# Attention scores for four heads at a time, in four row groups and four PSUM banks

## The chip, the cores and the metric

The kernel runs on one core of a Trainium2 chip. The metric is the device time in microseconds (us) of one execution. A profile is taken in an execution of its own. TensorE (PE in the profile) does matmuls and transposes into PSUM, which has eight banks of 2 KB per partition; VectorE (DVE) and ScalarE (ACT) read the banks and do the elementwise work; GpSimd (POOL) does elementwise work and gathers; SyncE (SP) issues transfers.

## The reference, cut to what matters

One block of a gated cross-attention layer, over 8 batches of 256 rows with 512 columns:

```python
x = x + tanh(g_xattn) * xattn(layernorm(x), ctx, mask, ...)
x = x + tanh(g_ffn) * ffn(layernorm(x), ...)

# xattn: 16 heads of 32 columns; q and the output go through int8-quantised products
q = w8a8_linear(x, wq, bq)      # heads: B, 16, 256, 32
k = cond @ wk.T + bk            # B, 16, 256, 32
v = cond @ wv.T + bv
scores = q @ k.T / sqrt(32) + mask
o = softmax(scores) @ v
return w8a8_linear(o, wo, bo)
```

The feed-forward part quantises its input and weights to an fp8 grid, with permuted columns, and computes `silu(g) * u` and a product down. The change touches only the attention.

## The kernel before

The program is written as a sequence of operations on tiles; a planner lays out each engine's queue from it, with priorities that follow the program's order, a cost of its own for each operation, and the buffers of each pool; it also sets the semaphores. A queue runs strictly in the order that was laid out. `tc.keep_in_program_order` pins an instruction behind the one written before it on its engine; that keeps an order, but doesn't keep other instructions out from between. `tc.high_priority()` raises the priority of what is written inside it.

First come the weights' transposes and quantisation and the projections of batch 0 (up to about 60 us), then the eight batches of attention (to about 560 us), then the feed-forward part, which uses PSUM pools of its own.

For each batch, `attention` walks over NP = 8 pairs of heads in a pipeline of turns. In turn i it writes down:

- `scores(i)`: for both heads of pair i and both row tiles of 128 queries, one matmul of K = 32 rows (a head's 32 columns lie on 32 partitions, so a head occupies one of four row groups of the array), with 256 keys as output columns. Both heads' scores go into one PSUM slot `s` of two banks, a bank per head; the pool `ps_s` has one such slot. Then, per head and row tile, VectorE adds the mask, writes `sn` and takes the row's extreme (L537), and ScalarE writes the exponentials `pr` with their sum (L547). `sn` has two buffers, `pr` four.
- `transposed(i - 1)`: per head four transposes of `pr` (L563) into a bank of the pool `ps_t` (two banks), and a copy to `pT` by VectorE for even heads (L572), by ScalarE for odd ones (L570).
- `weighted(i - 2)`: products of `v` and `pT` (L583) into a bank of `ps_o`, 32 output partitions per head; after every second pair `normalised` transposes and scales four heads' results (L596 to L605).
- a share of the list `others`.

`others` is the side work of the batch, handed out evenly over the 11 turns: the previous batch's output projection and its quantisation for the feed-forward part (`project_out`, `quantise_x2`), the next batch's projections (`project_kv` with the lines L414 to L445, `project_q` with L462 to L493), and pieces of the feed-forward weights' preparation (`prep_up`, `prep_down`; the helpers at L162 to L184 and L281 to L284). All that these write on TensorE goes through `bank`, the pool `ps_m` of three banks. So PSUM is split into 2 banks for scores, 2 for transposes of the exponentials, 1 for weighted sums and 3 for everything else.

Of the kernel before, what the change touches and what calls it, by code (L numbers as in the profile page):

```python
# [29 lines left out]
F32 = mybir.dt.float32  # L30
# [7 lines left out]
PSUM = bass.MemoryType.PSUM  # L38
DRAM = bass.MemoryType.DRAM

P = 128
# [10 lines left out]
def tile_flamingo_block(  # L52
# [133 lines left out]
    with ExitStack() as actx:  # L186
# [3 lines left out]
        at = actx.enter_context(tc.tile_pool(name="at", bufs=2))  # L190
# [1 line left out]
        one = actx.enter_context(tc.tile_pool(name="one", bufs=1))  # L192
        sm = actx.enter_context(tc.tile_pool(name="sm", bufs=4))
        ps_s = actx.enter_context(tc.tile_pool(name="ps_s", bufs=1, space=PSUM))
        ps_t = actx.enter_context(tc.tile_pool(name="ps_t", bufs=2, space=PSUM))
        ps_o = actx.enter_context(tc.tile_pool(name="ps_o", bufs=1, space=PSUM))
        ps_m = actx.enter_context(tc.tile_pool(name="ps_m", bufs=3, space=PSUM))

        def bank(name, dt=F32):
            n = 512 if dt == F32 else 1024  # L200
            return ps_m.tile([P, n], dt, tag="m", name=name)
# [84 lines left out]
        def load_rows(n, w, tag):  # L286

            tiles = []
            for k in range(KC):
                wr = at.tile([P, C], F32, tag=tag, name=f"wr_{n}{k}", bufs=4)  # L290
# [208 lines left out]
        def attention(b, qT, kT, v, mk, others):  # L499
# [7 lines left out]
            probs, probsT, poT = {}, {}, {}  # L507
            NP = H // 2
            PPC = HPC // 2

            def in_turn(first, ins):

                if not first:
                    tc.keep_in_program_order(ins)

            def scores(i):
                heads = (2 * i, 2 * i + 1)
                both = ps_s.tile([P, 2, TPB, L], F32, tag="s", name=f"s_{b}_{i}")
                pss = {h: both[:, h % 2] for h in heads}
                for nt in range(TPB):  # L520
                    for h in heads:
                        oc, r0 = h // HPC, (h % HPC) * D
                        ins = nc.tensor.matmul(  # L523
                            pss[h][:, nt, :],
                            qT[r0 : r0 + D, oc, nt * P : (nt + 1) * P],
                            kT[r0 : r0 + D, oc, :],
                            start=True,
                            stop=True,
                        )
                        in_turn(nt == 0 and h == heads[0], ins)  # L530
                for h in heads:
                    sn = at.tile([P, TPB, L], F32, tag="sn", name=f"sn_{b}_{h}")
                    pr = at.tile([P, TPB, L], F32, tag="pr", name=f"pr_{b}_{h}", bufs=4)
                    nm = sm.tile([P, TPB], F32, tag="nm", name=f"nm_{b}_{h}")

                    for nt in range(TPB):
                        nc.vector.tensor_tensor_reduce(  # L537
                            out=sn[:, nt, :],
                            in0=pss[h][:, nt, :],
                            in1=mk[:, nt, :],  # L540
                            scale=-1.0,
                            scalar=3.0e38,
                            op0=ALU.add,
                            op1=ALU.min,
                            accum_out=nm[:, nt : nt + 1],
                        )
                        nc.scalar.activation(  # L547
                            pr[:, nt, :],
                            sn[:, nt, :],
                            AF.Exp,  # L550
                            bias=nm[:, nt : nt + 1],
                            scale=-1.0,
                            accum_out=sums[:, nt, h : h + 1],
                        )
                    probs[h] = pr

            def transposed(i):
                for h in (2 * i, 2 * i + 1):
                    pr = probs.pop(h)
                    pst = ps_t.tile([P, LC, S], F32, tag="t", name=f"t_{b}_{h}")  # L560
                    for nt in range(TPB):
                        for lc in range(LC):
                            nc.tensor.transpose(  # L563
                                pst[:, lc, nt * P : (nt + 1) * P],
                                pr[:, nt, lc * P : (lc + 1) * P],
                                ident,
                            )
                    pT = at.tile([P, LC, S], F32, tag="pT", name=f"pT_{b}_{h}", bufs=4)
                    if h % 2:
                        nc.scalar.copy(pT, pst)  # L570
                    else:
                        nc.vector.tensor_copy(pT, pst)  # L572
                    probsT[h] = pT

            def weighted(i):
                heads = (2 * i + 1, 2 * i)
                oc = i // PPC
                if i % PPC == 0:
                    poT[oc] = ps_o.tile([P, S], F32, tag="o", name=f"poT_{b}_{oc}")
                for lc in range(LC):  # L580
                    for h in heads:
                        r0 = (h % HPC) * D
                        ins = nc.tensor.matmul(  # L583
                            poT[oc][r0 : r0 + D, :],
                            v[:, lc, h * D : (h + 1) * D],
                            probsT[h][:, lc, :],
                            start=(lc == 0),
                            stop=(lc == LC - 1),
                        )
# [124 lines left out]
        kT, v, steps = project_kv(0, cr)  # L714
# [3 lines left out]
        qT, q_steps = project_q(0)  # L718
# [215 lines left out]
```

## Time and profile before

| | us |
|---|---|
| median of 3 runs | 800.9 (799.37 to 805.62) |
| the profiled execution | 801.53 |
| its span, from the first to the last instruction | 799.8 |
| TensorE, matmuls | 624.2 busy (78%), 3560 records |
| TensorE, weight loads | 381.3 busy (48%) |
| VectorE | 537.3 busy (67%) |
| ScalarE | 414.3 busy (52%) |
| GpSimd | 279.3 busy (35%) |
| mean granted TensorE clock | 0.86 |

In the lines of the profile, a group of instructions is given as line, engine, operation, output<-inputs, then shapes and count; behind the first bar stand its busy time in us (overlapping instructions counted once) and the mean ns of one; behind the second the idle time of the engine just before the group, and what ended most of it. A row of 40 digits cuts the span into slices of 20 us; a digit is the busy share in tenths. In a table of windows a row is a stretch of the span with its length, the busy time of each engine in it and the number of its instructions, the granted clock, the transfers' share and GB/s. In a timeline a row gives start and duration in us, then the instructions merged.

### The profile page before, as it was taken

What the parts mean: (1) busy time and instruction counts of PE and PEld (TensorE: products, weight loads), DVE (VectorE), ACT (ScalarE), POOL (GpSimd) and SP (SyncE); (2) the same over time, 40 slices, a digit from 0 to 9 for tenths busy, and PEclk for the clock granted to TensorE, in tenths of its full rate; (3) what the DMA queues carried; (4) which work ended last, traced back from release to release, by engine and by line L of the source; (5) the groups of instructions that cost most, each with busy time, mean ns of one, the idle gap of its engine ahead of it and who ended that gap; (6) DMA issues with size and microseconds to landing.
All of it is one profiled execution on the core that took longest, in us unless ns stands there. A gap on an engine that the chain in (4) does not pass through costs nothing. (4 is left out here: it accounts for less than half of the span.)

```text
span 799.8 us, 10417 instructions
## 1 busy us (share of the span) xinstructions
PE 624.2 (78%) x3560; PEld 381.3 (48%) x3584; DVE 537.3 (67%) x1427; ACT 414.3 (52%) x959; POOL 279.3 (35%) x241
## 2 busy tenths in 40 slices
PE   3781798799898898899999889785576686777862
PEld 3640465555465465475575465453263343344431
DVE  3952776848747757756764766995566679778871
ACT  3441964656564665574483475674224544435540
POOL 3523343251141342143121310033545665564531
PEclk9885898998799899799699799678598989989986
DMA  9722130120022220021010411131110010010000
GB/s 290 251 15 12 36 104 27 28 65 14 2 80 85 74 82 25 1 66 41 0 54 14 145 39 46 39 100 47 36 31 26 27 40 27 27 40 27 27 14 26
DMA packets 27157, 42.59 MB, mean 53 GB/s; under 512 B 6528, under 2 KB 14080, under 8 KB 27104
## 3 DMA queue, kind: packets, MB, share of 16 engines
q1 hardware_dynamic: 18656, 29.17, 11.3%
q0 software_dynamic: 4864, 12.22, 5.8%
q10 hardware_dynamic: 3584, 0.54, 0.4%
q8 instruction: 28, 0.46, 0.2%
q14 instruction: 25, 0.20, 0.1%
HBM read 31.28 MB, written 10.63 MB: 52 GB/s over the span
## 5 line engine op out<-in xcount | busy, mean ns | idle before, releaser
L547 ACT ACTIVATE pr<-sn,nm 128x256 f32<-128x256 f32 x256 | 127.4, 499 | 115.8 <-DVE nm L537 91.9
L523 PE MATMUL s<-kT,qT 32*128 32x256 f32 x512 | 99.0, 473 | 44.7 <-DVE nm L537 40.2
L563 PE MATMUL t<-ident,pr 128*128 128x128 f32 x512 | 94.0, 321 | 23.6 <-ACT pr L547 10.8
L537 DVE CUSTOM_DVE_ANT_0 sn<-s,mk 128x256 f32<-128x256 f32 x256 | 96.6, 416 | 15.6 <-PE s L523 14.2
L523 PEld LDWEIGHTS s<-kT,qT 32*128 32x128 f32 x512 | 55.2, 216 | 79.1 <-DVE nm L537 39.4
L563 PEld LDWEIGHTS t<-ident,pr 128*128 128x128 f32 x512 | 66.6, 163 | 51.8 <-ACT pr L547 32.6
L824 PEld LDWEIGHTS <-xg 128*128 128x128 bf16 x512 | 52.6, 104 | 74.8 <-issue 34.9
L856 POOL TENSOR_TENSOR tt<-up,sl 128x704 f32<-128x704 f32 x32 | 62.9, 1966 | 39.6 <-DVE up L846 24.1
L583 PE MATMUL poT<-pT,v 128*32 128x256 f32 x512 | 73.0, 408 | 0.0
L824 PE MATMUL p_up<-upT,xg 128*128 128x352 bf16 x256 | 51.9, 340 | 21.1 <-DVE up L846 18.5
L424 PE MATMUL pk<-cT,wkT 128*128 128x256 f32 x256 | 58.7, 383 | 2.5 <-ACT cT L417 2.5
L824 PE MATMUL p_gate<-gateT,xg 128*128 128x352 bf16 x256 | 48.8, 335 | 14.2 <-DVE gs L837 7.4
L664 POOL TENSOR_TENSOR x_sb<-x_sb,bo_b 128x512 f32<-128x512 f32 x16 | 23.1, 1453 | 101.9 <-ACT xq L462 101.8
L438 PE MATMUL pv<-wvT,cT 128*128 128x512 f32 x128 | 57.1, 598 | 0.2 <-ACT wvT L268 0.2
L665 POOL TENSOR_TENSOR x_sb<-x_sb,y 128x512 f32<-128x512 f32 x16 | 20.2, 1270 | 97.2 <-DVE y L661 65.8
L493 POOL TENSOR_SCALAR qT<-qT,bq_c 128x256 f32<-128x256 f32 x32 | 19.0, 603 | 99.3 <-DVE qT L490 98.9
L424 PEld LDWEIGHTS pk<-cT,wkT 128*128 128x128 f32 x256 | 47.4, 190 | 12.0 <-ACT cT L417 4.2
L184 DVE TENSOR_REDUCE mxt<-tt 128x1 f32<-128x1408 f32 x16 | 25.9, 1619 | 33.9 <-POOL tt L856 33.9
L547 ACT ACTIVATION_READ_ACCUMULATOR pr<-sn,nm 128x1 f32 x256 | 48.0, 188 | 0.0
L572 DVE COPY pT<-t 128x512 f32<-128x512 f32 x64 | 43.7, 683 | 3.4 <-PE t L563 2.8
L874 PE MATMUL yp<-wdT,qtT 128*128 128x512 bf16 x161 | 41.5, 405 | 5.2 <-ACT qtT L871 3.1
L871 ACT COPY qtT<-ptq 128x1024 bf16<-128x1024 bf16 (+1 forms) x32 | 22.3, 749 | 42.8 <-PE ptq L868 42.8
(184 smaller groups left out, 1187.5 us busy)
## 6 DMA issues: line engine op xcount, KB each, us to landing
cr<-in_ctx_dram SPq DMA_DIRECT2D x8, 512.0 KB, 3.9
x_sb<-in_x_dram SPq DMA_DIRECT2D x8, 512.0 KB, 8.5
out_dram<-yo SPq DMA_DIRECT2D x16, 256.0 KB, 2.0
wd<-in_L_ffn_w_down_dram SPq DMA_DIRECT2D x4, 704.0 KB, 4.0
mk<-in_mask_BxSxS_ff_dram SPq DMA_DIRECT2D x8, 256.0 KB, 2.6
scr_x<-x2T SPq DMA_DIRECT2D x8, 256.0 KB, 4.0
scr_gate<-gateT SPq DMA_DIRECT2D x1, 1408.0 KB, 5.2
scr_up<-upT SPq DMA_DIRECT2D x1, 1408.0 KB
```

What stands on the lines that cost most here:

```text
L184: nc.vector.tensor_reduce(dst, src, AX.X, ALU.max, apply_absolute_value=True)
L424: nc.tensor.matmul(pk[:, :L], wTf["k"][:, cc, oc * P : (oc + 1) * P], cT[:, cc, :], start=(cc == 0), stop=(cc == KC - 1),)
L438: nc.tensor.matmul(pv, cT[:, cc, lt * P : (lt + 1) * P], wTf["v"][:, cc, :], start=(cc == 0), stop=(cc == KC - 1),)
L523: ins = nc.tensor.matmul(pss[h][:, nt, :], qT[r0 : r0 + D, oc, nt * P : (nt + 1) * P], kT[r0 : r0 + D, oc, :], start=True, stop=True,)
L537: nc.vector.tensor_tensor_reduce(out=sn[:, nt, :], in0=pss[h][:, nt, :], in1=mk[:, nt, :], scale=-1.0, scalar=3.0e38, op0=ALU.add, op1=ALU ...
L547: nc.scalar.activation(pr[:, nt, :], sn[:, nt, :], AF.Exp, bias=nm[:, nt : nt + 1], scale=-1.0, accum_out=sums[:, nt, h : h + 1],)
L563: nc.tensor.transpose(pst[:, lc, nt * P : (nt + 1) * P], pr[:, nt, lc * P : (lc + 1) * P], ident,)
L572: nc.vector.tensor_copy(pT, pst)
L583: ins = nc.tensor.matmul(poT[oc][r0 : r0 + D, :], v[:, lc, h * D : (h + 1) * D], probsT[h][:, lc, :], start=(lc == 0), stop=(lc == LC - 1),)
L824: nc.tensor.matmul(ph[n][:, j, :QI], xg[:, k, nt * P : (nt + 1) * P], wT[n][:, k, c0 : c0 + QI], start=(k == 0), stop=(k == KC - 1),)
L856: nc.gpsimd.tensor_tensor(tt[:, cols], up, sl, ALU.mult)
L874: nc.tensor.matmul(py, qT[:, k, :], wdT[:, k, :], start=(k == 0), stop=(k == IC - 1))
```

## The change

The pool of two transpose banks is given up; `s` becomes a slot of four banks, still a single one; the transposes take banks from the pool of three. `scores(i)` now covers four heads, which lie in the four row groups, and is called in every second turn. The products of a run go through a new `in_turn`: the first is written as it comes, all later ones at high priority and pinned behind each other. `weighted` uses the same `in_turn`, with two heads as before. Transposes come two turns after the turn of their pair instead of one, the weighted sums three instead of two, and there are 12 turns instead of 11. `pr` gets six buffers. `load_rows`, which loads wv and wq into the buffers of `pT` and `pr`, takes the number of buffers as an argument.

```diff
         ps_s = actx.enter_context(tc.tile_pool(name="ps_s", bufs=1, space=PSUM))
-        ps_t = actx.enter_context(tc.tile_pool(name="ps_t", bufs=2, space=PSUM))
         ps_o = actx.enter_context(tc.tile_pool(name="ps_o", bufs=1, space=PSUM))
         ps_m = actx.enter_context(tc.tile_pool(name="ps_m", bufs=3, space=PSUM))
...
-            def in_turn(first, ins):
-
-                if not first:
-                    tc.keep_in_program_order(ins)
+            def in_turn(products):
+
+                products[0]()
+                with tc.high_priority():
+                    for product in products[1:]:
+                        tc.keep_in_program_order(product())
 
             def scores(i):
-                heads = (2 * i, 2 * i + 1)
-                both = ps_s.tile([P, 2, TPB, L], F32, tag="s", name=f"s_{b}_{i}")
-                pss = {h: both[:, h % 2] for h in heads}
-                for nt in range(TPB):
-                    for h in heads:
-                        oc, r0 = h // HPC, (h % HPC) * D
-                        ins = nc.tensor.matmul(
-                            pss[h][:, nt, :],
-                            qT[r0 : r0 + D, oc, nt * P : (nt + 1) * P],
-                            kT[r0 : r0 + D, oc, :],
-                            start=True,
-                            stop=True,
-                        )
-                        in_turn(nt == 0 and h == heads[0], ins)
+                heads = range(i * HPC, (i + 1) * HPC)
+                four = ps_s.tile([P, HPC, TPB, L], F32, tag="s", name=f"s_{b}_{i}")
+                pss = {h: four[:, h % HPC] for h in heads}
+
+                def product(nt, h):
+                    r0 = (h % HPC) * D
+                    return nc.tensor.matmul(
+                        pss[h][:, nt, :],
+                        qT[r0 : r0 + D, i, nt * P : (nt + 1) * P],
+                        kT[r0 : r0 + D, i, :],
+                        start=True,
+                        stop=True,
+                    )
+
+                in_turn([partial(product, nt, h) for nt in range(TPB) for h in heads])
                 for h in heads:
                     sn = at.tile([P, TPB, L], F32, tag="sn", name=f"sn_{b}_{h}")
-                    pr = at.tile([P, TPB, L], F32, tag="pr", name=f"pr_{b}_{h}", bufs=4)
+                    pr = at.tile([P, TPB, L], F32, tag="pr", name=f"pr_{b}_{h}", bufs=6)
...
             def transposed(i):
                 for h in (2 * i, 2 * i + 1):
                     pr = probs.pop(h)
-                    pst = ps_t.tile([P, LC, S], F32, tag="t", name=f"t_{b}_{h}")
+                    pst = bank(f"t_{b}_{h}").rearrange("p (c n) -> p c n", n=S)
...
-                for lc in range(LC):
-                    for h in heads:
-                        r0 = (h % HPC) * D
-                        ins = nc.tensor.matmul(
...
-                        in_turn(lc == 0 and h == heads[0], ins)
+                in_turn([partial(product, lc, h) for lc in range(LC) for h in heads])
...
-            last = NP + 2
+            last = NP + 3
             given = 0
             for i in range(last + 1):
-                if i < NP:
-                    scores(i)
-                if 0 <= i - 1 < NP:
-                    transposed(i - 1)
+                if i < NP and i % PPC == 0:
+                    scores(i // PPC)
                 if 0 <= i - 2 < NP:
-                    weighted(i - 2)
-                    if (i - 2) % PPC == PPC - 1:
-                        normalised((i - 2) // PPC)
+                    transposed(i - 2)
+                if 0 <= i - 3 < NP:
+                    weighted(i - 3)
+                    if (i - 3) % PPC == PPC - 1:
+                        normalised((i - 3) // PPC)
...
-        rows_v = load_rows("v", wv, "pT")
-        rows_q = load_rows("q", wq, "pr")
+        rows_v = load_rows("v", wv, "pT", 4)
+        rows_q = load_rows("q", wq, "pr", 6)
```

More of the change, by code (lines that the diff above doesn't have):

```diff
@@ L284, in transpose_bf16, with load_rows @@
             nc.any.tensor_copy(dst, pt[:, : n * P].rearrange("p (k o) -> p k o", o=P))
-        def load_rows(n, w, tag):
+        def load_rows(n, w, tag, bufs):
             tiles = []
             for k in range(KC):
-                wr = at.tile([P, C], F32, tag=tag, name=f"wr_{n}{k}", bufs=4)
+                wr = at.tile([P, C], F32, tag=tag, name=f"wr_{n}{k}", bufs=bufs)
                 nc.sync.dma_start(wr, w[k * P : (k + 1) * P, :])
@@ L579, in weighted, with product @@
                     poT[oc] = ps_o.tile([P, S], F32, tag="o", name=f"poT_{b}_{oc}")
-                for lc in range(LC):
-                    for h in heads:
-                        r0 = (h % HPC) * D
[L583 to L589, printed above, removed]
-                        in_turn(lc == 0 and h == heads[0], ins)
+                def product(lc, h):
+                    r0 = (h % HPC) * D
+                    return nc.tensor.matmul(
+                        poT[oc][r0 : r0 + D, :],
+                        v[:, lc, h * D : (h + 1) * D],
+                        probsT[h][:, lc, :],
+                        start=(lc == 0),
+                        stop=(lc == LC - 1),
+                    )
+                in_turn([partial(product, lc, h) for lc in range(LC) for h in heads])
                 for h in heads:
```

## The prediction

> **What bounds the kernel now.** I read the page first, for where TensorE is full and which clock it had.
>
> ```profile
> PE   3781798799898898899999889785576686777862
> DVE  3952776848747757756764766995566679778871
> PEclk9885898998799899799699799678598989989986
> L547 ACT ACTIVATE pr<-sn,nm 128x256 f32<-128x256 f32 x256 | 127.4, 499 | 115.8 <-DVE nm L537 91.9
> L523 PE MATMUL s<-kT,qT 32*128 32x256 f32 x512 | 99.0, 473 | 44.7 <-DVE nm L537 40.2
> L537 DVE CUSTOM_DVE_ANT_0 sn<-s,mk 128x256 f32<-128x256 f32 x256 | 96.6, 416 | 15.6 <-PE s L523 14.2
> L583 PE MATMUL poT<-pT,v 128*32 128x256 f32 x512 | 73.0, 408 | 0.0
> ```
>
> A slice is 20 us. In slices 6 to 24 (the attention of batches 1 to 6) TensorE stands at 8 or 9 tenths, VectorE at 5 to 8, and the scores (L523) are TensorE's costliest line. The average hides two kinds of stretch, so I next asked for the busy time of each engine in windows of two consecutive batches, whole and then for L523 alone:
>
> ```profile
> core 0: us, PE busy (x) PEld busy (x) DVE busy (x) ACT busy (x) POOL busy (x), PEclk, DMA share, GB/s
> 311.00:337.00 26.00, 20.85 (x120) 12.04 (x119) 19.89 (x67) 13.73 (x41) 4.29 (x4) 0.80 0.00 1
> 337.00:374.00 37.00, 36.12 (x206) 23.90 (x204) 21.56 (x76) 22.97 (x63) 12.38 (x12) 0.91 0.20 58
> 374.00:400.00 26.00, 22.98 (x123) 12.73 (x122) 20.07 (x68) 13.18 (x40) 4.81 (x6) 0.74 0.00 1
> 400.00:437.00 37.00, 35.22 (x212) 23.07 (x210) 21.09 (x72) 22.22 (x61) 6.45 (x7) 0.95 0.13 37
> ...
> 311.00:337.00 26.00, 8.42 (x35) 4.58 (x37) 0.80 0.00 1
> 337.00:374.00 37.00, 4.93 (x32) 2.84 (x28) 0.91 0.20 58
> 374.00:400.00 26.00, 8.44 (x34) 4.37 (x36) 0.74 0.00 1
> 400.00:437.00 37.00, 4.33 (x34) 2.58 (x32) 0.95 0.13 37
> ```
>
> Each batch has an **open** stretch of 26 us (the previous batch's output projection and quantisation are its side work; TensorE 80 to 88% busy, at a clock of 0.74 to 0.80) and a **packed** stretch of 37 us (the next batch's keys, values and queries; TensorE 95 to 98% busy, VectorE under 60%). Four of the eight score pairs fall in each. What a score pair looks like, from the timeline of TensorE, first packed at full clock, then open:
>
> ```profile
> 347.93 1.13 PE L523 MATMUL s<-kT,qT 32*128 32x256 f32 x8
> 348.99 1.10 PE L563 MATMUL t<-ident,pr 128*128 128x128 f32 x8
> 350.02 1.06 PE L583 MATMUL poT<-pT,v 128*32 128x256 f32 x8
> ...
> 317.49 2.08 PE L523 MATMUL s<-kT,qT 32*128 32x256 f32 x8
> 319.50 1.03 PE L642 MATMUL ot<-ident_b,qo 128*128 128x128 bf16 x8
> 320.33 1.27 PE L563 MATMUL t<-ident,pr 128*128 128x128 f32 x5
> 321.53 2.07 PE L523 MATMUL s<-kT,qT 32*128 32x256 f32 x6
> ```
>
> A product is two MATMUL records, so a pair (2 heads, 2 row tiles) is 8. One record lasts 375 ns by the median, eight take 1.13 us: they run two abreast, one per row group. At the low clock it is 2.08. The last run above is cut: its last two records come at 326.88, behind the output projection. In the packed stretch the score bank pair lies free for 5 to 9 us between pairs and TensorE itself is the limit. In the open stretch it is reloaded at once: VectorE ends the reductions of the pair of 317.49 at 321.18 and the next scores start at 321.53. There the loop scores, reductions, scores is a limit beside TensorE's slow clock.
>
> **What the Trainium skill says.** "TensorE: Matmul & The Clock Gate", Part 3 (packing small matmuls): matmuls in different row groups run concurrently, their starts about 4 ns apart, and four row tiles measured 3.07 times the speed. The trace agrees for two: the two records of a step start 6 to 7 ns apart. Four are not shown. The same page, Part 1: the array's clock is halved after a window without enough activity, and full again after a busy one. The trace shows it: the granted clock alternates between 1.0 and 0.5, and in batches 2 to 6 each drop follows a stretch with waits of 0.7 us or more. "TensorEngine Tiling (Array Packing)", Gotcha 1 (PSUM Pressure): different row tiles must write different banks, which is why four heads need a slot of four.
>
> **The change, part by part.**
>
> Scores. 64 runs of 8 become 32 runs of 16. Four abreast, a step of the present run (0.31, 0.21, 0.21 and a last 0.37 us between starts and end, sum 1.13 with the offsets) holds four records instead of two; two more offsets of 7 ns per step make 1.13 + 4 x 0.014 = 1.18 us per run at full clock and 2.14 at half. The packed stretch has 4.93 and 4.33 us of L523 per batch, mean 4.6; two runs of 1.18 are 2.4. **Saved 2.2 us, x 7 batches with projections = 16 us**, all on the path, because TensorE has nearly no gap there. The open stretch has 8.4 us; two runs of 2.14 are 4.3: 4.1 us saved on TensorE. TensorE idles 3 to 5 us of 26 there and VectorE is 77% busy, so I count half: **2.1 x 7 = 15 us** (bounds 0 and 29). For the first batch, which waits for setup, and the last, where VectorE is nearly without gaps from 507 to 542, **3 us** together. Sum 34 of the at most 54 us that L523 can lose (99.0 less 32 runs at a mean of 1.4).
>
> In_turn. All products after the first are put at high priority, so a run is no longer cut by other work: the cut run of 321.53 and those at 311, 384 and 446 have 2.07 to 3.3 us of records instead of 1.13 to 2.08. This is inside the sums above, since L523's busy time was used. For the weighted sums (L583) it changes nothing: 61 of 64 stand in whole runs of 8 already, two abreast; they stay two heads. Cost 0.
>
> Reductions. Eight in a row instead of four on VectorE, at 0.344 us pitch: 2.75 us instead of 1.38 between the scores and the freeing of the slot, but half as many handovers. `sn` keeps two buffers: the third head's reduction waits for the first head's exponentials. ScalarE gives one per 0.49 us, so two are ready 1.5 us after the first reduction began, against 1.38 us when VectorE gets there: 0.1 us if ScalarE is free, up to 1 us if a 0.6 to 1.0 us copy stands before them. Behind the waiting reduction stands all of VectorE's queue. It matters in the open stretch and in the last batch, some 20 runs: bounds 2 and 20 us, partly covered by waits that VectorE has anyway; **I take 3.** Six `pr` buffers instead of four cover the four heads of a run and one pair before; cost 0, as the transposes that free the older ones are ready long before.
>
> Banks. The transposes lose their two banks and join the three of projections and preparation. To price it I paired each bank's first write with the end of its copy in the trace: from 120 to 480 us a transpose bank is held 3.4 us (1.8 of it waiting for the copying engine to come round), the others 2.0 us. More than three of the five are held during 4% of that time. Had the present order run on three banks, 28 of all tenures between 60 and 560 us would have found none free, and waited **23 us** together (8.6 the transposes, 14.3 the others). The order is laid out anew with three banks known, so other work can fill part; a lower bound is 0. **I take 8.**
>
> Later stages. Transposes run two turns behind the turn of their scores and weighted sums three, with 12 turns instead of 11, so side work is spread a little thinner. At a batch's end the next batch's work covers it. At the very end the last four heads' exponentials (8 x 0.49 = 3.9 us) stand before the last transposes; there TensorE now waits 7.3 us from 544.6 for VectorE anyway. Cost 0, 2 us if that cover is gone.
>
> Clock. With less to do in the open stretch TensorE has more gaps, and the clock falls on gaps. The open stretch already runs at 0.74 to 0.80; at 0.70 its remaining 17 us of matmul would take 1 to 2 us longer per batch, but only half counts: bounds 0 and 12, **I take 3.**
>
> The loads of the weights at the start use the same pools, with six buffers for wq: nothing to wait for. The feed-forward part from 570 us isn't touched.
>
> Sum: 34 - 3 - 8 - 3 = 20. The profiled execution took 801.5 us (span 799.8), 0.6 above the median of 800.9; 801.5 - 20 = 781.5, against the median **781 us**.
>
> **Rivals.** (1) *Bank pool, slower.* TensorE runs in order: where a transpose finds no bank, scores, projections and everything behind it wait. For it: transposes are 128 tenures of the longest waits, three banks are held or more 16% of the time, and the copies stand in long queues. Against it: the 23 us above. It decides once the mean stall per pair of transposes passes 28/64 = 0.44 us (34 saved, 6 for the other costs); at 0.75 us it costs 48 and gives **821**. (2) *Nothing in the end.* The packed stretch yields its 16, but the open one is held by VectorE's queue and the slower clock (0 of 15), and banks take 12: 801 - 4 = **797**. (3) *Not four abreast*: a run of 16 two abreast takes 0.31 + 6 x 0.21 + 0.37 = 1.96 us, 0.3 less than two runs; 10 us are saved over 32 runs at full clock, 14 lost as above: **805**. (4) *The whole 54 us* come through, since the loop in the open stretch shortens as well, less 6: **753**.
>
> **How the numbers follow.** Chances: forecast (764 to 793) 0.54; rival 1 0.20; rival 2 0.12; rival 3 0.06; rival 4 0.08. A measurement of this kernel tells 1% from no change, so faster means below 792.9 and slower above 808.9. Faster: 0.52 of the forecast and 0.08, 0.60. Slower: rival 1 and a third of rival 3, 0.22. Same: 0.18. For 8 in 10 the range takes in rivals 2 and 3 and the nearer half of rivals 1 and 4: 754 to 819.
>
> **What would show it.** Right: L523 in runs of 16 of about 1.2 us with busy time near 46 to 50, batch periods (62 us now) near 59 to 60, the packed stretch still without gaps. The step on banks is wrong if TensorE waits for copies (L570, L572, L431, L445) for more than 10 us between 120 and 480; that on reductions if VectorE's L537 waits for exponentials; that on the clock if the open stretch falls below 0.70. The prediction fails if the order that is laid out anew puts waits in the packed stretch, or if the open stretch grows by what the packed one loses.

## The result and the profile after

The changed kernel takes 874.6 us (872.23 to 880.87) against 801.7 us beside it: ratio 1.0916, 95% interval 1.0843 to 1.0989. It is slower by 9%, where a gain of 2.5% was forecast, and outside the predicted range of 754 to 819. Ratios here and below leave out single executions clearly slower than the others of their kernel (one of share_three at 1404.8 us, one of the kernel before at 817.2). Its profiled execution took 875.51 us, its span 873.7.

From the page of the changed kernel, rows of slices and groups (the scores are L524 now, the reductions L539, the exponentials L549, the transposes L565, the weighted sums L585):

```profile
PE   3814695677488589569649758744648767778772
DVE  3926737627836844863862774683647677778872
PEclk9976897799799679779869769957858898999986
L549 ACT ACTIVATE pr<-sn,nm 128x256 f32<-128x256 f32 x256 | 127.1, 498 | 84.4 <-DVE nm L539 70.3
L539 DVE CUSTOM_DVE_ANT_0 sn<-s,mk 128x256 f32<-128x256 f32 x256 | 96.3, 418 | 20.1 <-PE s L524 11.7
L585 PE MATMUL poT<-pT,v 128*32 128x256 f32 x512 | 74.0, 417 | 11.8 <-ACT pT L572 11.8
L524 PE MATMUL s<-kT,qT 32*128 32x256 f32 x512 | 45.5, 477 | 38.3 <-DVE so L178 16.4
```

The scores cost TensorE 45.5 us, where they cost 99.0, and TensorE is busy for 584 us instead of 624. Yet the 8s and 9s of TensorE's row have become a pattern of 4 to 9: holes in every batch. To place the loss I cut both spans at the first reduction of batches 0, 1 and 7 and at the last copy of attention (L596 before, L599 now). Windows of the kernel before, then of the changed one; the second column is the length:

```profile
47.40:131.40 84.00, 55.40 (x311) 33.98 (x308) 46.62 (x144) 46.83 (x115) 34.02 (x32) 0.82 0.21 44
131.40:507.40 376.00, 337.36 (x1940) 210.01 (x1946) 252.61 (x844) 219.43 (x613) 90.50 (x88) 0.88 0.15 46
507.40:556.80 49.40, 38.16 (x230) 23.79 (x232) 38.77 (x131) 30.53 (x92) 13.23 (x13) 0.72 0.23 74
556.80:799.80 243.00, 162.43 (x930) 91.21 (x946) 168.07 (x218) 101.00 (x110) 122.79 (x82) 0.86 0.08 29
```

```profile
40.00:134.50 94.50, 52.94 (x331) 34.31 (x329) 51.91 (x164) 46.37 (x115) 32.26 (x32) 0.82 0.19 40
134.50:556.80 422.30, 301.90 (x1888) 192.13 (x1889) 256.91 (x826) 217.32 (x603) 87.33 (x85) 0.83 0.12 39
556.80:628.70 71.90, 38.76 (x287) 24.66 (x286) 47.70 (x145) 37.68 (x106) 15.15 (x16) 0.72 0.19 61
628.70:873.70 245.00, 166.83 (x946) 92.31 (x944) 167.37 (x216) 99.67 (x108) 122.68 (x82) 0.86 0.08 28
```

Of the 74 us, 46 are in the six middle batches (422.3 against 376.0; 70 us a batch instead of 63), 22 in the last batch, 3 before and in the first, 2 in the rest. In the middle TensorE has 35 us less to do and idles 120 us instead of 39. What it waits for, first the kernel before, then the changed one (the engine and its line, what for, us in total, times, the longest):

```profile
PE tb_x L281 <- DVE q L167: 6.5, 6, 2.6
```

```profile
PE tb_x L280 <- DVE q L167: 51.9, 14, 6.4
PE s L524 <- DVE so L178: 16.4, 6, 3.2
PE tb_d L280 <- DVE q_d L167: 14.5, 6, 6.7
DVE st L679 <- POOL x_sb L668: 16.5, 8, 12.6
```

52 us, 47 of them in the middle batches, go into waiting for `q`, the rows that `quantise_x2` has quantised, ahead of their transposes `tb_x`. The change touched neither the quantisation nor these transposes. One such place, on TensorE, in the changed kernel:

```profile
362.29 1.59 PE L565 MATMUL t<-ident,pr 128*128 128x128 f32 x8
363.81 1.15 PE L524 MATMUL s<-kT,qT 32*128 32x256 f32 x16
365.98 1.06 PE L585 MATMUL poT<-pT,v 128*32 128x256 f32 x8 [1.03 <-ACT pT L572]
370.57 0.61 PE L280 MATMUL tb_x<-ident_b,q 128*128 128x128 bf16 x4 [3.53 <-DVE q L167]
375.89 0.61 PE L280 MATMUL tb_x<-ident_b,q 128*128 128x128 bf16 x4 [4.71 <-DVE q L167]
376.29 1.92 PE L565 MATMUL t<-ident,pr 128*128 128x128 f32 x8
...
379.12 1.89 PE L565 MATMUL t<-ident,pr 128*128 128x128 f32 x8
```

From 367.04 to 376.29 TensorE runs nothing but two `tb_x`, and stands still for 8.2 us. The transposes of the next exponentials, whose inputs are there by 365 at the latest (the timeline of ScalarE), stand behind both. In the kernel before they stood ahead: there, in the same part of a batch, run

```profile
327.50 1.10 PE L563 MATMUL t<-ident,pr 128*128 128x128 f32 x8
...
332.20 1.09 PE L563 MATMUL t<-ident,pr 128*128 128x128 f32 x8
333.23 1.06 PE L583 MATMUL poT<-pT,v 128*32 128x256 f32 x8
334.46 0.40 PE L281 MATMUL tb_x<-ident_b,q 128*128 128x128 bf16 x4 [0.18 <-DVE q L167]
```

I counted for each batch how many pairs of heads have been transposed when its first and when its second `tb_x` starts (batches 1 to 6; a half pair is one head):

| kernel | banks of the transposes | ahead of the first | ahead of the second |
|---|---|---|---|
| before | own pool | 3 to 4 | 3.5 to 5 |
| changed | common | 1 (batch 6: 0) | 1 |

One and one is just the order in which the program writes them: 23 steps of side work over 12 turns put both `tb_x` into turn 2, behind the transposes of pair 0 and ahead of those of pair 1; in batch 6, with 24 steps, the first falls into turn 1, ahead of pair 0. My **theory**: tiles of one pool reach TensorE in the order written, since each takes over a bank from one written earlier. In a pool of their own the transposes overtake a `tb_x` that isn't ready; in a common one they can't, however many banks it has. The **rivals**: too few banks; the later turns; the slot of four banks, loaded in one piece.

### The profile page after: what moved, and what is told of

It is laid out like the page before. It is cut to its first block, busy times and chain, and to the rows that moved or that the text cites. A ratio compares the mean times of both kernels' runs of the same rounds, so it can differ in the third digit from the quotient of the medians.

```text
span 873.7 us, 10452 instructions
## 1 busy us (share of the span) xinstructions
PE 584.4 (67%) x3584; PEld 362.3 (41%) x3584; DVE 549.1 (63%) x1427; ACT 417.8 (48%) x959; POOL 276.2 (32%) x241
## 5 line engine op out<-in xcount | busy, mean ns | idle before, releaser
L549 ACT ACTIVATE pr<-sn,nm 128x256 f32<-128x256 f32 x256 | 127.1, 498 | 84.4 <-DVE nm L539 70.3
L539 DVE CUSTOM_DVE_ANT_0 sn<-s,mk 128x256 f32<-128x256 f32 x256 | 96.3, 418 | 20.1 <-PE s L524 11.7
L565 PE MATMUL t<-ident,pr 128*128 128x128 f32 x512 | 86.2, 317 | 28.6 <-DVE pT L574 24.8
L565 PEld LDWEIGHTS t<-ident,pr 128*128 128x128 f32 x512 | 71.2, 167 | 46.0 <-DVE pT L574 27.8
L585 PE MATMUL poT<-pT,v 128*32 128x256 f32 x512 | 74.0, 417 | 11.8 <-ACT pT L572 11.8
L524 PE MATMUL s<-kT,qT 32*128 32x256 f32 x512 | 45.5, 477 | 38.3 <-DVE so L178 16.4
L423 PE MATMUL pk<-cT,wkT 128*128 128x256 f32 x256 | 63.9, 402 | 6.7 <-ACT kT L430 3.1
L572 ACT COPY pT<-t 128x512 f32<-128x512 f32 x64 | 36.6, 573 | 47.8 <-PE t L565 47.8
L437 PE MATMUL pv<-wvT,cT 128*128 128x512 f32 x128 | 59.1, 609 | 0.0
L423 PEld LDWEIGHTS pk<-cT,wkT 128*128 128x128 f32 x256 | 49.9, 202 | 18.8 <-ACT cT L416 4.1
L524 PEld LDWEIGHTS s<-kT,qT 32*128 32x128 f32 x512 | 28.7, 224 | 50.9 <-issue 39.7
L877 PE MATMUL yp<-wdT,qtT 128*128 128x512 bf16 x176 | 46.5, 419 | 2.7 <-ACT qtT L874 2.7
L444 DVE TENSOR_TENSOR v<-pv,bv_b 128x512 f32<-128x512 f32 x16 | 11.0, 690 | 59.1 <-PE pv L437 59.1
L549 ACT ACTIVATION_READ_ACCUMULATOR pr<-sn,nm 128x1 f32 x256 | 48.1, 188 | 0.0
```

The lines of the kernel that those rows point to most:

```text
L423: nc.tensor.matmul(pk[:, :L], wTf["k"][:, cc, oc * P : (oc + 1) * P], cT[:, cc, :], start=(cc == 0), stop=(cc == KC - 1),)
L437: nc.tensor.matmul(pv, cT[:, cc, lt * P : (lt + 1) * P], wTf["v"][:, cc, :], start=(cc == 0), stop=(cc == KC - 1),)
L524: return nc.tensor.matmul(pss[h][:, nt, :], qT[r0 : r0 + D, i, nt * P : (nt + 1) * P], kT[r0 : r0 + D, i, :], start=True, stop=True,)
L539: nc.vector.tensor_tensor_reduce(out=sn[:, nt, :], in0=pss[h][:, nt, :], in1=mk[:, nt, :], scale=-1.0, scalar=3.0e38, op0=ALU.add, op1=ALU ...
L549: nc.scalar.activation(pr[:, nt, :], sn[:, nt, :], AF.Exp, bias=nm[:, nt : nt + 1], scale=-1.0, accum_out=sums[:, nt, h : h + 1],)
L565: nc.tensor.transpose(pst[:, lc, nt * P : (nt + 1) * P], pr[:, nt, lc * P : (lc + 1) * P], ident,)
```

## The experiments

In us, with the ratio to the kernel before; "common 3" is a pool of three banks for the transposes and everything else, "own 2+3" two for the transposes and three for the rest.

| kernel | heads | banks | median | ratio (95%) |
|---|---|---|---|---|
| share_five | 2 | common 5 | 859.2 | 1.070 (1.064 to 1.075) |
| share_three | 2 | common 3 | 856.2 | 1.065 (1.060 to 1.070) |
| two_own21 | 2 | own 1+2 | 835.5 | 1.041 (1.035 to 1.048) |
| four_own | 4 | own 1+2 | 847.8 | 1.052 (1.045 to 1.059) |
| four_flat | 4 | common 3 | 822.3 | 1.022 (1.018 to 1.027) |
| four_late | 4 | common 3 | 785.1 | 0.976 (0.972 to 0.980) |
| two_late | 2 | own 2+3 | 788.9 | 0.980 (0.976 to 0.985) |
| four_early | 4 | common 3 | 849.1 | 1.054 (1.050 to 1.059) |
| four_early_late | 4 | common 3 | 790.5 | 0.981 (0.977 to 0.985) |
| two_lag | 2 | own 2+3 | 788.9 | 0.983 (0.979 to 0.987) |
| two_in_turn | 2 | own 2+3 | 794.2 | 0.989 (0.985 to 0.992) |
| two_lag_turn | 2 | own 2+3 | 782.4 | 0.974 (0.969 to 0.978) |
| all_but_four | 2 | common 3 | 845.9 | 1.053 (1.047 to 1.058) |
| own21_all_but_four | 2 | own 1+2 | 822.1 | 1.022 (1.017 to 1.027) |
| two_lag_turn_late | 2 | own 2+3 | 777.8 | 0.968 (0.964 to 0.972) |
| four_late_mixed | 4 | common 3 | 778.2 | 0.968 (0.966 to 0.971) |
| four_deep | 4 | common 3 | 852.1 | 1.060 (1.055 to 1.065) |
| four_late_mixed_deep | 4 | common 3 | 768.9 | 0.956 (0.953 to 0.959) |

Differences between two kernels below are differences of ratios, times 801.5 us.

**The common pool alone.** In the kernel before, the transposes move into the common pool, which gets all five banks (share_five), or keeps three (share_three); the rest stays.

```diff
-        ps_t = actx.enter_context(tc.tile_pool(name="ps_t", bufs=2, space=PSUM))
-        ps_m = actx.enter_context(tc.tile_pool(name="ps_m", bufs=3, space=PSUM))
+        ps_m = actx.enter_context(tc.tile_pool(name="ps_m", bufs=5, space=PSUM))
...
-                    pst = ps_t.tile([P, LC, S], F32, tag="t", name=f"t_{b}_{h}")
+                    pst = bank(f"t_{b}_{h}").rearrange("p (c n) -> p c n", n=S)
```

> The kernel before (two-head slots, two banks, own turns), with one edit: the transposes of the exponentials draw from one common pool of five banks together with projections and quantisation, instead of two and three. Theory A (the common pool hands out its banks in written order, so transposes of exponentials must follow the transposes of the quantised rows (tb_x) in TensorE's queue, and TensorE stands still while VectorE is not ready with those): slower than before by 20 us or more, 820 to 860, with TensorE waiting for the quantised rows 25 us or more in total (about 8 before). Theory B (too few banks): the number of banks is unchanged, so 795 to 806. Theory C (the four-head slot and its eight reductions are to blame): 795 to 806.

> As the run with the common pool of five, with three banks only: the kernel before with the bank division of the changed kernel, scores still two heads in two banks. Theory A: within 8 us of the common pool of five. Theory B: slower than the common pool of five by 20 us or more. Theory C: 795 to 810.

859.2 and 856.2 us, +56 and +52. With not one bank fewer the loss is there, and two banks fewer add nothing. Batches 1 to 6 start their two `tb_x` behind 1 and 2 pairs, as written (11 turns), with either number of banks; in batches 2 to 6 the whole sequence of transposes and side work on TensorE is the same in both, record by record. The waits land elsewhere than in the changed kernel, though: TensorE waits for `q` only 15.3 us in share_five and 6.2 in share_three. It waits for the reductions:

```profile
PE s L522 <- DVE nm L536: 77.4, 27, 23.4
PE tb_x L280 <- DVE q L167: 15.3, 6, 8.7
```

(share_five; 40.2 and 6.5 us before. The longest of the waits for reductions, 23.4 us, lies at the start, as one of 19.4 does before.) With a slot of two banks the scores of further pairs are still issued; the reductions then need buffers of exponentials, which the transposes behind `tb_x` have to free. So the time bore the theory out, but the expectation of 25 us or more of waits for `q` was missed. The timeline of TensorE in share_five shows the chain:

```profile
290.93 1.13 PE L522 MATMUL s<-kT,qT 32*128 32x256 f32 x8 [1.22 <-DVE nm L536]
294.88 2.08 PE L522 MATMUL s<-kT,qT 32*128 32x256 f32 x8 [2.83 <-DVE nm L536]
296.89 0.61 PE L280 MATMUL tb_x<-ident_b,q 128*128 128x128 bf16 x4
297.30 1.92 PE L562 MATMUL t<-ident,pr 128*128 128x128 f32 x8
...
303.95 0.61 PE L280 MATMUL tb_x<-ident_b,q 128*128 128x128 bf16 x4
304.35 1.92 PE L562 MATMUL t<-ident,pr 128*128 128x128 f32 x8
```

The Trainium skill ("Perfetto Trace Analysis", Optimizing Tensor Performance, Matmuls) advises that independent groups of matmuls rotate through different PSUM banks, so that the eviction of one lies beside the next. That agrees with four_own below, where a pool of a single bank costs TensorE 53 us of waits for the copies that free it. The runs here add that what rotates together is tied in order as well.

**The same banks in pools of their own.** In the changed kernel the three banks are split again, one for the transposes and two for the rest (four_own); two_own21 does that in the kernel before.

```diff
+        ps_t = actx.enter_context(tc.tile_pool(name="ps_t", bufs=1, space=PSUM))
...
-        ps_m = actx.enter_context(tc.tile_pool(name="ps_m", bufs=3, space=PSUM))
+        ps_m = actx.enter_context(tc.tile_pool(name="ps_m", bufs=2, space=PSUM))
...
-                    pst = bank(f"t_{b}_{h}").rearrange("p (c n) -> p c n", n=S)
+                    pst = ps_t.tile([P, LC, S], F32, tag="t", name=f"t_{b}_{h}")
```

> The changed kernel with the three banks split again: one bank in a pool of its own for the transposes of the exponentials, two for all other work; scores, turns and side work as changed. Theory A: the order of the two kinds of transposes comes free again, 800 to 845 in spite of fewer banks for each. Theory B (too few banks): 875 or more.

> The kernel before with one bank for the transposes of the exponentials and two for the other work, in pools of their own. If the number of banks binds a two-head kernel with free order as it seemed to bind the four-head one with the same division (847.8): 825 to 850. Theory A' (banks in free order cost little, the rest of that run's loss is the four-head slot with its turns): 802 to 818.

four_own is 32 us faster than the changed kernel on the same three banks (847.8 us, 3 above the range of the theory): 2.5 pairs now stand ahead of the first `tb_x`. Here the number of banks does count: two_own21 is +33 us against its 2+3, and in four_own TensorE waits for the copies that free the single bank:

```profile
PE t L566 <- ACT pT L573: 36.8, 26, 3.1
PE t L566 <- DVE pT L575: 16.0, 15, 2.1
```

So there are two prices for the banks, order and number, and each split pays one of them.

**Taking away what `tb_x` waits for.** four_flat is the changed kernel with `tb_x` reading a constant tile in place of the quantised rows; the quantisation is still done, but the feed-forward part gets a constant input instead of the reference's.

```diff
+    flat = ctile([P, C], "flat", BF16)
+    nc.vector.memset(flat, 1.0)
...
-                transpose_bf16(q2, xT[:, :, nt * P : (nt + 1) * P], KC, f"x2_{t}")
+                transpose_bf16(flat, xT[:, :, nt * P : (nt + 1) * P], KC, f"x2_{t}")
```

> The changed kernel, but the transposes of the quantised rows (tb_x) read a constant tile, so they wait for nothing; the quantisation itself is still computed, the feed-forward input is not the reference's. Theory A: most of the loss is gone, 780 to 825. Theory B: TensorE still waits for banks, 850 or more. Theory C: 850 or more.

822.3 us: 55 of the 73 us are gone. The middle batches take 377.5 us, as before the change (376.0); the last batch stays at 71.4 (71.9).

four_late takes nothing away and only writes the quantisation's steps later, behind the keys and values of the next batch, so that its `tb_x` start behind five pairs (four for the first one in batch 6); two_late does the same in the kernel before.

```diff
                 others = after + kv_steps + q_steps + pieces[n0:n1]
+                if b > 0:
+                    others = after[:3] + kv_steps + after[3:] + q_steps + pieces[n0:n1]
```

> The changed kernel, with the quantisation of the rows (quantise_x2) written after the next batch's keys and values instead of before them in the list of side work; all work is done. Theory A: the chain of the quantisation is covered by the projections, 790 to 835. Theory B and C: 860 or more.

> The kernel before, with only the quantisation of the rows written after the next batch's keys and values. Theory A (in the kernel before the transposes run ahead of the quantised rows anyway, since they have their own pool): between 785 and 805, so the later quantisation alone gives little, and the four-head scores give the rest of what the run with both gained. Rival D (the later quantisation is a gain of its own and the four-head scores are worth nothing): within 5 us of 785.

four_late takes 785.1 us, 92 less than the changed kernel with the same work in the same banks, and the middle batches fall to 332.9 us; two_late gains 16. This is the same `tb_x` and the same common pool; what differs is the place in the written order. 785.1 is 5 us below the range of its theory, and 788.9 fits both ranges that were given for two_late. The two together tell more than each alone: they differ by the whole change, which is worth -3 us there (0.976 against 0.980, within what the intervals leave open) in place of +73. That makes the written order the main cause of the loss.

**Turns and in_turn.** four_early is the changed kernel with the transposes one turn behind their pair and the weighted sums two, as before (11 turns); four_early_late adds the late order. two_lag does the reverse in the kernel before, with six `pr` buffers; two_in_turn brings the new `in_turn` alone.

```diff
-            last = NP + 3
+            last = NP + 2
...
-                if 0 <= i - 2 < NP:
-                    transposed(i - 2)
-                if 0 <= i - 3 < NP:
-                    weighted(i - 3)
-                    if (i - 3) % PPC == PPC - 1:
-                        normalised((i - 3) // PPC)
+                if 0 <= i - 1 < NP:
+                    transposed(i - 1)
+                if 0 <= i - 2 < NP:
+                    weighted(i - 2)
+                    if (i - 2) % PPC == PPC - 1:
+                        normalised((i - 2) // PPC)
```

> The changed kernel with transposes one turn and weighted sums two turns behind their pair, and 11 turns, as in the kernel before; the pool stays common. Theory A: transposes of the next pair and a weighted sum now are written between the two quantised row tiles, so TensorE's waits for them fall to half or less: 810 to 850. If the later turns are not to blame at all: 865 to 885.

> The changed kernel with both: earlier turns and the quantisation of the rows written after the keys and values. Theory A: the chain is covered already by the later quantisation (785), so the earlier turns add little: 775 to 795. A larger gain would say that the three-turn pipeline costs by itself.

> The kernel before with only the later turns: transposes two and weighted sums three turns behind their pair, 12 turns, six pr buffers; banks, two-head slots and side work as before. Theory A' (the six middle batches lost by the common pool, the first and last batch by the later turns): the middle batches within 8 us of before in sum, the last batch longer by 8 to 20 us, total 805 to 825. If the later turns are free: 797 to 806.

> The kernel before with only the new way to write a run of products: all after the first at high priority, for scores and weighted sums, two heads at a time. Runs of scores are no longer cut. Forecast had priced this inside the scores' gain: cut runs give back 0.6 to 1.2 us in three places per batch, 790 to 803. If contiguity blocks work that was better placed between: 803 to 820.

The same turns have either sign. With the four-head slot in the common pool the later turns cost 30 us (849.1 against 874.6). They write the transposes behind one more `tb_x` there, but TensorE's waits for `q` only differ by 15 us (36.8 in four_early, not half of 51.9 as expected); the next sections show what else is in it. With the late order, where nothing stands ahead, the later turns gain 4 us, within what these two intervals leave open. In a pool of their own, where the written order binds nobody, they gain 14 us with the two more `pr` buffers (788.9, below both ranges of the expectation), and `in_turn` gains 9 (794.2).

**The change built up step by step.** two_lag_turn is the kernel before with the later turns and `in_turn`. all_but_four adds the common pool of three, and so is the whole change but for the four-head slot; own21_all_but_four has one and two banks in pools of their own instead. Their edits are those of the diffs above together.

> The kernel before with later turns, six pr buffers and runs at high priority, its own five banks and two-head slots: what of the change needs no banks. If the two gains add: 776 to 784. If they overlap: 784 to 792.

> Everything of the change except the four-head slot: common pool of three banks, later turns, runs at high priority, six pr buffers; scores stay two heads in two banks. If the later turns turn bad once the pool is common (order, not slot): 862 to 885, as the changed kernel, and the four-head slot is worth about nothing. If the parts add (856 - 14 - 9): 826 to 842, and the four-head slot costs 35 to 45 us.

> The kernel before with one bank for transposes and two for other work in pools of their own, later turns and runs at high priority; the run four_own (847.8) without the four-head slot. Order theory (slot not to blame): 840 to 855. Slot theory: 805 to 825 (835 - 14 - 9 = 812).

By the ratios 1, 0.9735, 1.0526, 1.0916: later turns and `in_turn` **-21 us**, common pool **+63**, four-head slot **+31**. With pools of their own the slot costs +24 as well (1.0218 to 1.0521). So half the scores' time on TensorE, taken away, came with a loss that the common pool alone doesn't explain.

These three numbers hold for this sequence of steps only. all_but_four, at 845.9 us, lies between its two ranges: later turns, `in_turn` and six `pr` together took 10 us off share_three (856.2), although share_three writes the transposes of its second pair ahead of the second `tb_x` and all_but_four doesn't. And with the earlier turns the four-head kernel (four_early, 849.1, with `in_turn` and six `pr`) is no slower than share_three. So the slot's +31 and the later turns' +30 look like one and the same cost, which comes when the two meet: with only one of them, beside `in_turn` and six `pr` in the common pool, no such cost is seen. The kernel with neither of them, but with these three, wasn't run, so the division isn't shown.

**What the slot costs.** In the changed kernel VectorE's reductions of 363.81 (timeline of VectorE, then of ScalarE) run like this:

```profile
367.07 0.41 DVE L539 CUSTOM_DVE_ANT_0 sn<-s,mk 128x256 f32<-128x256 f32 x1
...
368.22 0.42 DVE L539 CUSTOM_DVE_ANT_0 sn<-s,mk 128x256 f32<-128x256 f32 x1
...
380.27 0.69 DVE L574 COPY pT<-t 128x512 f32<-128x512 f32 x1 [0.53 <-PE t L565]
380.88 0.41 DVE L539 CUSTOM_DVE_ANT_0 sn<-s,mk 128x256 f32<-128x256 f32 x1
```

```profile
365.37 0.56 ACT L572 COPY pT<-t 128x512 f32<-128x512 f32 x1
...
379.18 0.49 ACT L549 ACTIVATE pr<-sn,nm 128x256 f32<-128x256 f32 x1
```

Four reductions, then 12 us until the fifth, while the slot of four banks stays taken. Its exponentials come at 379.18, after the transposes of 376.29, which free two `pr`. So a chain runs from `tb_x` over transposes, `pr` and `sn` to the slot: it is held 21 to 22 us in the third of the four runs of scores in a batch (batches 2 to 5). In four_early, whose transposes free the `pr` a turn earlier, it is held 13.2 us there. four_deep gives the changed kernel eight `pr`; one buffer instead of two for `x2T`, the transposed rows of the feed-forward, makes the room.

```diff
-                    pr = at.tile([P, TPB, L], F32, tag="pr", name=f"pr_{b}_{h}", bufs=6)
+                    pr = at.tile([P, TPB, L], F32, tag="pr", name=f"pr_{b}_{h}", bufs=8)
...
-            xT = at.tile([P, KC, S], BF16, tag="x2T", name=f"x2T_{b}")
+            xT = at.tile([P, KC, S], BF16, tag="x2T", name=f"x2T_{b}", bufs=1)
...
-        rows_q = load_rows("q", wq, "pr", 6)
+        rows_q = load_rows("q", wq, "pr", 8)
```

> The changed kernel with eight buffers for the exponentials instead of six (room for them is made by one buffer fewer for the transposed rows of the feed-forward). Theory A, the second four reductions of a turn wait for buffers of exponentials whose transposes stand behind the quantised rows' transposes on TensorE, and so hold the four-bank slot some 21 us in each third turn: 845 to 862 us. Theory B, the four-bank slot costs its 25 to 31 us elsewhere (scores that come late in one piece, the last batch): 868 to 880 us.

852.1 us, 25 less; the smaller `x2T` wasn't tried by itself. The eight reductions of the third run now take 5.4 us from first to last, where they took 17.9. The wait for `q` is still there:

```profile
PE tb_x L280 <- DVE q L167: 42.7, 12, 7.4
```

What is left of the slot's cost, 1.060 against all_but_four's 1.053, is within what the two intervals leave open.

**Is there a version that wins?** two_lag_turn_late adds the late order to two_lag_turn. four_late_mixed is four_late with the earlier turns in the first and last batch only; four_late_mixed_deep adds the eight `pr`.

```diff
-            last = NP + 3
+            lag = 1 if b in (0, B - 1) else 2
+            last = NP + 1 + lag
...
-                if 0 <= i - 2 < NP:
-                    transposed(i - 2)
+                if 0 <= i - lag < NP:
+                    transposed(i - lag)
...
```

> As two_lag_turn, with the quantisation of the rows written after the keys and values. Against four_late (785) and four_late_mixed (778) it tells what four-head scores with three banks are worth against two-head scores with five. If four heads are worth the 16 us of the packed stretch: 790 or more. If nothing: 770 to 785.

> The changed kernel with the quantisation of the rows written after the keys and values, and with the turns of the kernel before (one and two behind) in the first and last batch only. Theory A': the first and last batch give back 8 to 20 of the 33 us that they lost there against the kernel before: 765 to 778. If their loss is the four-head slot itself: 782 to 788.

> The late order of the quantised rows with mixed lags, and eight buffers for the exponentials. Theory A, buffers of exponentials bind here too: 765 to 774 us. Theory B, they bind only where transposes stand behind the quantised rows: 775 to 782 us.

777.8, 778.2 and 768.9 us. four_late_mixed is 6 us faster than four_late, where 8 to 20 were expected. The last of the three beats both kernels, by 4.4% and 12%. Its page:

```profile
PE   3851786897996996996997983755667778678762
PEclk9995989798998997998997996765698899989985
L524 PE MATMUL s<-kT,qT 32*128 32x256 f32 x512 | 43.9, 464 | 19.0 <-DVE so L178 15.8
```

TensorE is busy 561 us there and 605.5 in two_lag_turn_late; the 44 us between them are worth 10 us of time, and without the eight buffers nothing. The two also differ in their banks (common 3 against own 2+3) and in the turns of the first and last batch. What bounds them wasn't tried; nor was a two-head kernel with the late order and eight `pr`, so the 10 us can't be split between heads and buffers.

## Why the prediction was wrong

**Scores: right.** 32 runs of 16; a run takes 1.15 us at full clock (1.18 was forecast) and 2.09 at half (2.14), L524 45.5 us in all ("near 46 to 50"). Rival 3, not four abreast, is excluded. That each row group needs a bank of its own, as the prediction takes it, no run here tests. The step from there to 34 us saved is another matter: with six `pr`, the 53.5 us that L523 lost brought a loss of 31 us (the slot in the common pool, later turns) or about nothing (late order: 778.2 against 777.8). Counting the packed stretch's 2.2 us in full "because TensorE has nearly no gap there" took a full engine for the bound of the batch.

**Banks: the step that failed.** It paired tenures of banks on the order of before, got 23 us at most and took 8, expecting the new order to fill part. The measured price is +52 us (share_three), or +63 on top of the later turns (all_but_four). It isn't the count that was mis-sized: with five banks the price is the same. The common pool changes the order itself, and the order can't be read off a pairing on the old one. In pools of their own the number does cost: 33 us for two banks fewer, above the 23 of the pairing.

The tell-tale named for this step, TensorE waiting more than 10 us for copies between 120 and 480, is there by its letter, with some 14 us, but not by its reason: 9.4 of them are weighted sums waiting for their input `pT`, and transposes, which were to find no bank, wait 1.2 us. The large wait is for `q`, a row of VectorE that no bank holds (39 us in that window). The last sign, waits in the packed stretch or a longer open one, came in both parts: TensorE is busy 33.0 of the 38 us from 376 to 414 (packed) and 16.3 of the 31 us before them (open), where the prediction's windows had 95 to 98% and 80 to 88%.

**Reductions, and the six `pr`: wrong.** "Cost 0, as the transposes that free the older ones are ready long before": their inputs are ready, by 365 at the latest, but their place on TensorE is behind two `tb_x`, until 376.29. With eight buffers 25 us come back, where 3 was taken and 20 was the upper bound for the whole step. The sign named for it came: in the middle batches VectorE's reductions wait 7.9 us for exponentials, in 13 places.

**Later stages: cost 0 was wrong either way.** -14 us with the transposes in their own pool (two_lag, with the two more `pr`), +30 in the common pool with the four-head slot (four_early). **In_turn** at 0 beyond the sums left out 9 us of gain in the kernel before.

**Clock.** 0.835 in the mean instead of 0.860, and in the middle batches 0.83 instead of 0.88. The Trainium skill ("TensorE: Matmul & The Clock Gate", Part 1) ties a low clock to a window of little activity. The middle batches agree (TensorE busy 90% at 0.88, 71% at 0.83), but the mean busy share doesn't settle it: from 134 to 454 us four_late_mixed_deep has 0.92 at 86%, two_lag_turn_late 0.89 at 90%, and the last batch has 0.72 both at 77% (before) and at 54% (changed). No run tried the clock as a cause.

**The last batch** was to gain a little; it lost 22 us. The trace shows a chain on GpSimd: eleven gathers of down weights, one after the other, start 26 us into the batch before and 36 us after the change, behind weight transposes (`tb_d`) the last of which starts 10 us later (28.6 against 18.2). The addition to `x_sb` follows them, and VectorE, with reductions and copies of the last heads in its queue, waits 12.6 us for that (the row `st` above). four_early has the gathers at 26 us and a last batch of 56.2; four_flat, without the wait for `q`, keeps 71.4. So the later turns have a part in it, but neither they nor late gathers suffice: two_lag, with the later turns, has a last batch of 52.5 us, and two_lag_turn_late starts its gathers at 37.8 us and takes 44.5. The chain was read off, not tried by itself, and how the 22 us divide stays open.

**The rivals.** Rival 1 had the side, and the place in part: the pool of banks. Its mechanism, a transpose that finds no bank, wasn't what happened, and its 821 is 54 us short.

Summed up, in the sequence of steps that was run: -21 us from turns and `in_turn`, +63 from the common pool's order, +31 from the slot where it meets the later turns, of which eight `pr` give 25 back: +73, against the -20 of the forecast.

## What to carry to other kernels

Before you merge two pools of PSUM, write down the order in which the program asks for their tiles: with the planner of this kernel, in common pools of three and of five banks, TensorE's queue got them in that order, and a tile whose input was late held up those behind it that were ready. Count what stands ahead of a late tile, not only the banks. When producers get a bigger slot, follow the chain of buffers (`sn`, `pr`, bank) to the instruction that frees the last of them, and see what it is queued behind.

## What the runs showed of the hardware beyond this

Four row groups with fp32 operands of K = 32 run nearly without loss: 16 records took 1.15 us where 8, two abreast, took 1.13. The step from two to four abreast is thus worth a factor of 1.97 here; the Trainium skill ("TensorE: Matmul & The Clock Gate", Part 3) lists 3.07 as the measured speedup of four row tiles with 512 columns, which can't be set beside this step, as no run here shows one row group alone. And TensorE's busy time was a poor guide to the time of this kernel: share_three is 21 us faster than the changed kernel, though its scores take twice as long and its TensorE is busy 636.5 us in place of 584.4.
